# A graph layer's last stage: a place of its own for every chunk of x

## The chip, the core and the metric

The kernel runs on one core of a Trainium2 chip. A core has five engines with queues of their own: TensorE (PE, matrix products and transposes), VectorE (DVE), ScalarE (ACT), GpSimd (POOL, here the issuer of gathers) and SyncE (SP, here the issuer of plain loads and stores). 16 DMA engines move data between the device memory and the on-chip memory SBUF, which has 128 partitions. An issuing engine works through its queue in order: a load that has to wait for its place holds back all that stands behind it.

The metric is the time of one execution on the device, in microseconds (us).

## The reference

`x` is a table of 12,500 nodes with 256 float32 features; `src` and `dst` list 200,000 edges, sorted by `dst`.

```python
h = maximum(layernorm(x), 0)                      # per row, no scale or shift
agg = segment_sum(h[src], dst, num_segments=N)    # sum over incoming edges
z = (1 + eps_gin) * h + agg
t = relu(batchnorm(z @ W1 + b1, g1, bt1))         # 256 -> 512, statistics over all nodes
y = t @ W2 + b2                                   # 512 -> 256
out = x + relu(batchnorm(y + h, g2, bt2))         # statistics over all nodes
```

Each batch norm needs the whole table's mean and variance before one row of its result can be made. So the work falls into three stages: gather and first layer, second layer, and output.

## The kernel before, in words

The 12,500 rows are cut into 25 chunks of 512 rows (`chunks`; the last has 212). The transposed form of a chunk puts features on the partitions.

**First stage** (lines 341 to 600, an order written out by hand under `manual_schedule`). It normalizes rows of x, gathers rows by edge with indirect DMAs from GpSimd (line 435, 12 tiles of 128 edges to a group, 131 groups), sums them by destination with products against a 0/1 matrix (L464, L478), and forms the first product in slices (L514). The product goes untransformed to a device table `t_tab` (1 MB a chunk), its statistics into `st1`; the transposed h lies in a device table `h_cols`. Five landing places for gathered groups rotate. Two of them are permanent pairs `lands[k] = (gta, gtb)`, of 8 KB and 4 KB on each partition; the others, `gt`, come from a pool. `dstT` and `srcT` (6,656 bytes on each partition) hold the edges' target and source indices, `w1s` and `w2s` (4 KB each) the two weights. All of these are permanent.

**Second stage** (L623 to L642). For each chunk SP loads the stored product into `ti` (one of three buffers of 8 KB) and the transposed h into `yT[g]`, of which every chunk has its own. ScalarE applies batch norm and relu into `tT`, which lies in the two `gta` in turn; TensorE multiplies by `w2s` (L637, 16 matmuls a chunk), VectorE adds h (L641) and takes statistics (L642). The last chunk is worked ahead of the one before it.

**Last stage** (L654 to L672). For each chunk ScalarE applies the second batch norm (L657), TensorE transposes back (L663), VectorE adds the result onto the rows of x in place (L668), and SP stores them to `out` (`carry`, L328). The rows of x, 4 KB on each partition for a chunk, have been loaded before by SP (`x_rows`, L330).

Where the 25 chunks of x lie: chunks 0 to 7 in the pool `xin` (8 places), 8 and 9 in the two `gtb`, 10 to 15 in the pool `xmore` (6 places, in the space of the `ti` buffers). Chunks 16 to 23 reuse the places of 0 to 7, and chunk 24 that of chunk 16. Such a load waits until the store of the place's former chunk has landed; it is traced three chunks behind that store.

Outside the first stage the order on each queue is made by a planner at build time: it places what its model of time holds ready, the earlier line of the program first. A load whose place is free early can thus come ahead of loads that stand before it in the program. The two `gtb` loads did: their place was free when the gathers had ended.

The functions that the diff touches:

Of the kernel before, what the change touches and what calls it, by code (L numbers as in the profile page):

```python
# [7 lines left out]
F32 = mybir.dt.float32  # L8
# [6 lines left out]
P = 128  # L15
R = 4
# [4 lines left out]
LEAD = 30  # L21
EARLY = 2
LOW = 8
XAHEAD = 10
XMORE = 6


# [6 lines left out]
def kernel(  # L34
# [16 lines left out]
    nc = tc.nc  # L51
    N, D = x.shape
# [5 lines left out]
    NCH = -(-N // CH)  # L58
# [24 lines left out]
    def move(eng, sb, table, g, store):  # L83
# [23 lines left out]
    srcT = consts.tile([P, NBLK * P], I32, name="srcT")  # L107
    dstT = consts.tile([P, NBLK * P], F32, name="dstT")
# [6 lines left out]
    lands = [  # L115
        (consts.tile([P, LOW, D], F32, name=f"gta{k}"), consts.tile([P, GT - LOW, D], F32, name=f"gtb{k}"))
        for k in range(EARLY)
    ]
# [18 lines left out]
    w1s = consts.tile([P, DC, H], F32, name="w1s")  # L137
    w2s = consts.tile([P, HC, D], F32, name="w2s")
# [5 lines left out]
    at = 0  # L144
# [6 lines left out]
    with ExitStack() as es:  # L151
# [54 lines left out]
        place = raw.tile([P, NG], I32, name="place")  # L206
# [47 lines left out]
        at = 0  # L254
# [52 lines left out]
    def fast():  # L307

        parts = []
        for n0, w in chunks:  # L310
            n = w * R
            parts.append([(c, min(P, n - c * P)) for c in range(-(-n // P))])

        def pieces(g):

            whole = sum(rows == P for _, rows in parts[g])
            yield 0, whole, P
            for c, rows in parts[g][whole:]:
                yield c, c + 1, rows

        def carry(eng, sb, table, g, store):
            n0 = chunks[g][0]
            for c0, c1, rows in pieces(g):
                if c0 == c1:
                    continue
                side = table[n0 + c0 * P : n0 + (c1 - 1) * P + rows, :].rearrange("(c p) d -> p c d", p=rows)
                if store:
                    eng.dma_start(side, sb[:rows, c0:c1, :])  # L328
                else:
                    eng.dma_start(sb[:rows, c0:c1, :], side)  # L330

        with ExitStack() as fs:
            keep = fs.enter_context(tc.tile_pool(name="keep", bufs=1))

            h_cols = dram.tile([NCH, P, DC, CH], F32, name="h_cols")
# [5 lines left out]
            with ExitStack() as es:  # L341
# [188 lines left out]
                def first(c):  # L530

                    return min(i for i in range(NG) if c in reach(i))
# [11 lines left out]
                for c in range(NCH):  # L544
                    k = max(first(c) + 1, c + 2)
# [59 lines left out]
            late = fs.enter_context(tc.tile_pool(name="late", bufs=1, reuse_waits="tile"))  # L605
            yT = [late.tile([P, DC, w * R], F32, name=f"yT{g}") for g, (_, w) in enumerate(chunks)]

            xin = fs.enter_context(tc.tile_pool(name="xin", bufs=XAHEAD - EARLY, reuse_waits="tile"))
            xrs = []

            def x_rows(g):
                if g < NCH:
                    if XAHEAD - EARLY <= g < XAHEAD:
                        xrs.append(lands[g - XAHEAD + EARLY][1])
                    else:
                        pool = xmore if XAHEAD <= g < XAHEAD + XMORE else xin
                        xrs.append(pool.tile([P, R, D], F32, name="xr"))
                    carry(nc.sync, xrs[g], x, g, store=False)


            with tc.tile_pool(name="tin", bufs=3, side="right", reuse_waits="tile") as tin, tc.tile_pool(name="ps_y", bufs=4, space=PSUM) as ps_y:

                for k, g in enumerate([*range(NCH - 2), NCH - 1, NCH - 2]):  # L623
                    n = chunks[g][1] * R
                    ti = tin.tile([P, HC, CH], F32, name="ti")
                    nc.sync.dma_start(ti[:, :, :n], t_tab[g, :, :, :n])
                    nc.sync.dma_start(yT[g], h_cols[g, :, :, :n])
                    tT = lands[k % EARLY][0].rearrange("p a d -> p (a d)").rearrange("p (f n) -> p f n", n=CH)
                    for f in range(HC):
                        nc.scalar.activation(  # L630
                            tT[:, f, :n], ti[:, f, :n], AF.Relu, bias=of1[:, f : f + 1],
                            scale=sc1[:, f : f + 1],
                        )
                    for d in range(DC):
                        py = ps_y.tile([P, CH], F32, name="py")
                        for f in range(HC):
                            nc.tensor.matmul(  # L637
                                py[:, :n], lhsT=w2s[:, f, d * P : (d + 1) * P], rhs=tT[:, f, :n],
                                start=(f == 0), stop=(f == HC - 1),
                            )  # L640
                        nc.vector.tensor_add(yT[g][:, d, :], py[:, :n], yT[g][:, d, :])  # L641
                        nc.vector.bn_stats(st2[:, d, g, :], yT[g][:, d, :])  # L642
                for g in range(XAHEAD):
                    x_rows(g)

            sc2, of2 = norm(late, st2, mv2, DC, g2c, bt2c, b2c, "2")

# [1 line left out]
            with tc.tile_pool(name="xmore", bufs=XMORE, side="right", reuse_waits="tile") as xmore, tc.tile_pool(  # L649
                name="ps_o", bufs=3, space=PSUM  # L650
            ) as ps_o:
                for g in range(XAHEAD, XAHEAD + XMORE):
                    x_rows(g)
                for g in range(NCH):  # L654
                    xt = xrs[g]
                    for d in range(DC):
                        nc.scalar.activation(  # L657
                            yT[g][:, d, :], yT[g][:, d, :], AF.Relu, bias=of2[:, d : d + 1], scale=sc2[:, d : d + 1]
                        )
                    po = ps_o.tile([P, R, D], F32, name="po")  # L660
                    for c, rows in parts[g]:
                        for d in range(DC):
                            nc.tensor.transpose(  # L663
                                po[:rows, c, d * P : (d + 1) * P], yT[g][:, d, c * P : c * P + rows], ident
                            )
                    for c0, c1, rows in pieces(g):
                        if c0 < c1:
                            nc.vector.tensor_add(xt[:rows, c0:c1, :], po[:rows, c0:c1, :], xt[:rows, c0:c1, :])  # L668
                    carry(nc.sync, xt, out, g, store=True)

                    if g >= 3:
                        x_rows(g - 3 + XAHEAD + XMORE)  # L672

    def general():

# [214 lines left out]
    with tc.If(off == 0):  # L890
        fast()
# [32 lines left out]
```

## Time and profile before

| | |
|---|---|
| median of 3 runs | 2235.57 us (2233.42 to 2241.05) |
| the profiled execution | 2235.88 us |
| its span, first to last instruction | 2233.7 us |
| mean granted TensorE clock | 0.834 |

| stretch, us | what | TensorE busy | ScalarE busy | share of the DMA engines | GB/s |
|---|---|---|---|---|---|
| 0 to 1960 | first stage: gathers | 1249.45 us | 387.88 us | | |
| 1960 to 2000.5 | first stage's end | 31.23 us | 8.25 us | 0.29 | 98 |
| 2000.5 to 2170.2 | second stage | 169.63 us | 78.76 us | 0.67 | 239 |
| 2170.2 to 2178.2 | second batch norm, first output chunk | 3.49 us | 4.88 us | 0.22 | 71 |
| 2178.2 to 2233.7 | last stage from its first store on | 24.85 us | 30.29 us | 0.92 | 312 |

A line of the profile names an engine, a line of the kernel (L657 is line 657), the tile written and, behind an arrow, what is read. "x6" is a count. PE is TensorE's matmuls; SPq is the SP queue, where the time of a DMA line is that of its issue, not of its transfer. "Idle" stands with what ended it: `[0.82 <-DMA ...]` says that the engine waited 0.82 us and a DMA released it. The chain that ended last is followed back from the last instruction, at each step to what released it. The share of the DMA engines is a mean over 16; values over 1 come from transfers that overlap on one engine.

### The profile page before, as it was taken

Reading aid. Unit: us, or ns where it says so; the run is one execution under the profiler, and the core shown is the slowest. Engines: PE = TensorE matmul, PEld = TensorE weight load, DVE = VectorE, ACT = ScalarE, POOL = GpSimd, SP = SyncE. Lnnn points to the kernel's source line nnn. Section 1 sums busy time; section 2 is a strip of 40 time slices with the busy share of each in tenths; the row PEclk is TensorE's granted clock in tenths of the full one; section 3 lists DMA queues with packets and bytes.
Section 4 is the critical chain, followed back from the end, with each engine's and each line's share of the span. In section 5 each row is a group of like instructions: output and inputs, shape, how many; then the busy total and the mean of one; then the engine's idle time right before and its main releaser. Section 6 shows DMA issues by size and latency. Waiting matters only on the chain.

```text
span 2233.7 us, 15142 instructions
## 1 busy us (share of the span) xinstructions
PE 1478.6 (66%) x4874; PEld 1066.5 (48%) x4874; DVE 716.5 (32%) x1092; ACT 510.1 (23%) x963; POOL 1480.4 (66%) x1575
## 2 busy tenths in 40 slices
PE   3567677667666666656666666666666666679994
PEld 2455545545444544544454444444444544444443
DVE  5566656531222122122212221211221121124345
ACT  4666666520000000000000000000000000034445
POOL 7777777777777777777777777777777777700000
PEclk9888888888888788878877887888887788789998
DMA  6677767644444444444444444444443444438739
GB/s 196 208 228 232 246 218 237 183 128 120 129 128 129 116 128 129 120 123 129 131 116 125 132 120 125 129 117 126 129 133 113 126 128 118 130 131 320 252 118 311
DMA packets 157615, 349.47 MB, mean 156 GB/s; under 512 B 30104, under 2 KB 82452, under 8 KB 154454
## 3 DMA queue, kind: packets, MB, share of 16 engines
q0 software_dynamic: 75008, 204.90, 32.8%
q1 hardware_dynamic: 54224, 104.03, 13.9%
q10 hardware_dynamic: 28294, 39.47, 4.9%
q8 instruction: 41, 0.67, 0.1%
q14 instruction: 48, 0.39, 0.1%
HBM read 284.28 MB, written 64.00 MB: 156 GB/s over the span
## 4 chain that ended last, share of the span: by engine, by line
POOL 52%; issue 22%; PE 11%; ACT 6%; DVE 4%; DMA 4%; ACTq 0%; SPq 0%; DVEq 0%; POOLq 0%
POOL gt L435 32%; POOL gta L435 12%; PE py L637 8%; POOL gtb L435 6%; DMA gt<-in_x_dram,srcT 3%; ACT gt L381 2%; DVE stg L370 2%; PE ps L478 2%; PE ph L514 1%; ACT yT L657 1%; ACT gta L381 1%; DMA out_dram<-xr 1%; DVE oh L464 1%; POOL gta L212 1%; ACT gtb L381 0%
## 5 line engine op out<-in xcount | busy, mean ns | idle before, releaser
L478 PE MATMUL ps<-gt,oh 128*128 128x256 f32 x1872 | 577.0, 481 | 402.5 <-DMA gt<-h_tab,srcT 321.5
L435 POOL DMA_INDIRECT gt<-h_tab,srcT x720 | 680.7, 945 | 219.3 <-issue 219.3
L478 PEld LDWEIGHTS ps<-gt,oh 128*128 128x128 f32 x1872 | 459.1, 250 | 546.0 <-issue 315.7
L478 PE MATMUL ps<-gta,oh 128*128 128x256 f32 x838 | 291.9, 524 | 270.5 <-DMA gta<-h_tab,srcT 212.1
L478 PEld LDWEIGHTS ps<-gta,oh 128*128 128x128 f32 x838 | 224.8, 275 | 352.4 <-issue 198.3
L525 DVE BATCH_NORM_STATS2 st<-ph 128x6 f32<-128x512 f32 (+1 forms) x100 | 68.4, 684 | 971.2 <-PE ph L514 971.2
L435 POOL DMA_INDIRECT gta<-h_tab,srcT x323 | 305.2, 945 | 98.4 <-issue 95.9
L527 ACT COPY ts<-ph 128x512 f32<-128x512 f32 (+1 forms) x100 | 57.4, 574 | 1326.5 <-DVE st L525 1326.5
L435 POOL DMA_INDIRECT gt<-in_x_dram,srcT x216 | 204.2, 945 | 65.8 <-issue 60.9
L464 DVE TENSOR_TENSOR oh<-col,dstT 128x1536 f32<-128x1536 f32 x131 | 227.7, 1738 | 0.0
L514 PE MATMUL ph<-zc,w1s 128*128 128x512 f32 (+1 forms) x400 | 193.1, 610 | 20.6 <-DVE hc L423 20.1
L507 DVE TENSOR_TENSOR zc<-pz,zc 128x512 f32<-128x512 f32 (+8 forms) x187 | 93.9, 520 | 282.5 <-PE pz L496 244.2
L435 POOL DMA_INDIRECT gtb<-h_tab,srcT x160 | 151.2, 945 | 48.7 <-issue 47.5
L637 PE MATMUL py<-gta,w2s 128*128 128x512 f32 (+1 forms) x400 | 169.6, 587 | 3.7 <-ACT gta L630 3.7
L496 PE MATMUL pz<-at,zs 128*128 128x256 f32 x524 | 134.9, 380 | 5.0 <-ACT zs L485 5.0
L637 PEld LDWEIGHTS py<-gta,w2s 128*128 128x128 f32 x400 | 76.4, 192 | 96.4 <-issue 75.7
L514 PEld LDWEIGHTS ph<-zc,w1s 128*128 128x128 f32 x400 | 78.3, 199 | 79.8 <-issue 49.1
L381 ACT ACTIVATE gt<-gt,nbg,rsg 128x256 f32<-128x256 f32 x216 | 108.1, 586 | 9.1 <-DVE nbg L379 8.1
L496 PEld LDWEIGHTS pz<-at,zs 128*128 128x128 f32 x524 | 97.6, 190 | 19.1 <-ACT zs L485 7.1
L630 ACT ACTIVATE gta<-ti,of,sc 128x512 f32<-128x512 f32 (+1 forms) x100 | 79.6, 803 | 82.9 <-PE py L637 78.8
L478 PE MATMUL ps<-gtb,oh 128*128 128x256 f32 x416 | 98.3, 379 | 0.0
L435 POOL DMA_INDIRECT gta<-in_x_dram,srcT x80 | 75.6, 946 | 24.4 <-issue 8.5
(97 smaller groups left out, 897.3 us busy)
## 6 DMA issues: line engine op xcount, KB each, us to landing
t_tab<-ts ACTq DMA_DIRECT2D x96, 256.0 KB
ti<-t_tab SPq DMA_DIRECT2D x24, 1024.0 KB
xt<-in_x_dram SPq DMA_DIRECT2D x24, 512.0 KB
h_tab<-ht ACTq DMA_DIRECT2D x24, 512.0 KB
h_cols<-hc SPq DMA_DIRECT2D x24, 512.0 KB
zc<-h_cols SPq DMA_DIRECT2D x24, 512.0 KB
yT<-h_cols SPq DMA_DIRECT2D x24, 512.0 KB
gt<-h_tab,srcT POOLq DMA_INDIRECT x720, 2.8
```

Of the source, the lines that this page charges most:

```text
L370: nc.vector.bn_stats(st[:, c : c + 2, :].rearrange("p c s -> p (c s)"), two.rearrange("p c d -> p d c"),)
L381: nc.scalar.activation(slot(to, c), slot(v, c), AF.Relu, bias=nb[:, c : c + 1], scale=rs[:, c : c + 1])
L435: nc.gpsimd.indirect_dma_start(out=slot(ga, t - t0)[:rows], out_offset=None, in_=x if i < LEAD else h_tab, in_offset=bass.IndirectOffsetOn ...
L464: nc.vector.tensor_tensor(ohs[i][:, :n, :], col[:, :P].unsqueeze(1).to_broadcast([P, n, P]), dstT[:, t0 : t0 + n].unsqueeze(2).to_broadcas ...
L478: nc.tensor.matmul(ps, lhsT=oh[:rows, j, :], rhs=slot(ga, j)[:rows], start=(j == 0), stop=(j == n - 1))
L496: nc.tensor.matmul(pz[:, d, :], lhsT=zs[:, d * P : (d + 1) * P], rhs=at, start=True, stop=True)
L507: nc.vector.tensor_add(side, pz[:, :, a - lo : b - lo], side)
L514: nc.tensor.matmul(ph[:, :n], lhsT=w1s[:, d, f * P : (f + 1) * P], rhs=zc[c][:, d, :n], start=(d == 0), stop=(d == DC - 1),)
L525: nc.vector.bn_stats(st1[:, f, c, :], ph[:, :n])
L527: nc.scalar.copy(ts[:, :n], ph[:, :n])
L630: nc.scalar.activation(tT[:, f, :n], ti[:, f, :n], AF.Relu, bias=of1[:, f : f + 1], scale=sc1[:, f : f + 1],)
L637: nc.tensor.matmul(py[:, :n], lhsT=w2s[:, f, d * P : (d + 1) * P], rhs=tT[:, f, :n], start=(f == 0), stop=(f == HC - 1),)
```

## The change

All 25 chunks of x now have a place of their own, and no load of x waits for a store.

- Chunks 0 to 7 stay in `xin`, 8 and 9 in the two `gtb`.
- Chunks 10, 11 and 12 lie in `dstT`, `srcT` (taken as float32) and `w1s`; the last chunk, 24, in the rest of `dstT`.
- All of these loads are traced after the second stage's loop, as the ten of before were, but within `issue_after(begun)`: on SP they stand behind the load of `yT` for the third chunk. This is an order of issue, no wait for a landing.
- Chunks 13 to 18 lie in `xmore`.
- Chunks 19 to 22 lie in the halves of the two `gta`, that of the second-to-last worked chunk first; chunk 23 in `w2s`. Their loads are traced right behind those of `xmore`, ahead of the output loop.
- The refill at the end of each turn of the output loop is gone.

```diff
-XAHEAD = 10
+XIN = 8
 XMORE = 6
...
-            xin = fs.enter_context(tc.tile_pool(name="xin", bufs=XAHEAD - EARLY, reuse_waits="tile"))
-            xrs = []
-
-            def x_rows(g):
-                if g < NCH:
-                    if XAHEAD - EARLY <= g < XAHEAD:
-                        xrs.append(lands[g - XAHEAD + EARLY][1])
-                    else:
-                        pool = xmore if XAHEAD <= g < XAHEAD + XMORE else xin
-                        xrs.append(pool.tile([P, R, D], F32, name="xr"))
-                    carry(nc.sync, xrs[g], x, g, store=False)
+            xin = fs.enter_context(tc.tile_pool(name="xin", bufs=XIN, reuse_waits="tile"))
+            xrs = {}
+
+            def rows_in(flat, at=0, c=R):
+                return flat[:, at : at + c * D].rearrange("p (c d) -> p c d", d=D)
+
+            def x_rows(places):
+                for g, place in places:
+                    xrs[g] = place
+                    carry(nc.sync, place, x, g, store=False)
...
-                    nc.sync.dma_start(yT[g], h_cols[g, :, :, :n])
+                    landing = nc.sync.dma_start(yT[g], h_cols[g, :, :, :n])
+                    if k == 2:
+                        begun = landing.ins
...
-                for g in range(XAHEAD):
-                    x_rows(g)
+                behind = [lands[k][1] for k in range(EARLY)]
+                behind += [rows_in(dstT), rows_in(srcT.bitcast(F32)), rows_in(w1s.rearrange("p a b -> p (a b)"))]
+                with tc.issue_after(begun):
+                    x_rows([(g, xin.tile([P, R, D], F32, name="xr")) for g in range(XIN)])
+                    x_rows(enumerate(behind, XIN))
+                    x_rows([(NCH - 1, rows_in(dstT, R * D, len(parts[NCH - 1])))])
...
-                for g in range(XAHEAD, XAHEAD + XMORE):
-                    x_rows(g)
+                got = len(xrs) - 1
+                x_rows([(g, xmore.tile([P, R, D], F32, name="xr")) for g in range(got, got + XMORE)])
+                last = [lands[k][0][:, c : c + R, :] for k in reversed(range(EARLY)) for c in range(0, LOW, R)]
+                last += [rows_in(w2s.rearrange("p a b -> p (a b)"))]
+                assert got + XMORE + len(last) == NCH - 1
+                x_rows(enumerate(last, got + XMORE))
...
                     carry(nc.sync, xt, out, g, store=True)
-
-                    if g >= 3:
-                        x_rows(g - 3 + XAHEAD + XMORE)
```

## The prediction

> **What bounds the kernel now.** I read the chain that ended last in order of time, then the SyncE (SP) queue's own timeline, then the load of the DMA engines in chosen windows. The chain past 2000 us (start us, us, what):
>
> ```profile
> 2000.51 169.65 PE py L637 x400
> ...
> 2201.49 15.93 DMA out_dram<-xr x2
> 2217.43 2.96 DMA xr<-in_x_dram
> ```
>
> TensorE alone sets the second layer: 169.65 us without a gap, up to 2170.2. After it the chain is DMA: a 15.93 us wait for a store to land, then the load that takes its place. The queue that issues both (start us, us taken by the issues):
>
> ```profile
> 1902.93 17.32 SPq L330 DMA_DIRECT2D gtb<-in_x_dram  x2
> 1984.64 5.99 SPq L627 DMA_DIRECT2D yT<-h_cols  x3
> 2002.60 0.32 SPq L626 DMA_DIRECT2D ti<-t_tab  x1
> ...
> 2161.34 3.98 SPq L330 DMA_DIRECT2D xr<-in_x_dram  x6
> 2178.23 5.50 SPq L328 DMA_DIRECT2D out_dram<-xr  x4
> ...
> 2200.22 1.22 SPq L330 DMA_DIRECT2D xr<-in_x_dram  x1
> 2201.49 12.22 SPq L328 DMA_DIRECT2D out_dram<-xr  x8
> ...
> 2218.35 8.31 SPq L328 DMA_DIRECT2D out_dram<-xr  x7
> ```
>
> Loads and stores alternate from 2183 to 2201. Seven stores stand behind the load of 2217.43, the last chunk's, which waits for the store of the chunk that held its place. The windows (stretch, busy time by engine, granted clock, share of the 16 DMA engines, GB/s):
>
> ```profile
> core 0 of [0], span 2233.7 us
> 2017.00:2100.00 83.00, 83.00 (x195) 36.84 (x194) 33.86 (x49) 39.19 (x49) 0.00 (x0) 1.00 0.88 319
> 2100.00:2161.00 61.00, 61.00 (x146) 27.41 (x145) 24.18 (x36) 27.98 (x36) 0.00 (x0) 1.00 0.33 111
> 2164.00:2170.00 6.00, 6.00 (x15) 2.45 (x13) 2.32 (x4) 0.00 (x0) 0.00 (x0) 1.00 1.07 351
> 2172.00:2178.00 6.00, 3.29 (x14) 3.00 (x15) 2.43 (x8) 4.68 (x8) 0.00 (x0) 0.53 0.01 2
> 2178.00:2229.50 51.50, 25.05 (x184) 20.02 (x182) 28.83 (x26) 30.49 (x44) 0.00 (x0) 0.83 0.99 337
> 2180.00:2184.00 4.00, 3.36 (x27) 2.66 (x26) 4.00 (x4) 4.00 (x7) 0.00 (x0) 1.00 0.94 314
> 2184.00:2188.00 4.00, 3.05 (x24) 2.34 (x23) 3.46 (x4) 4.00 (x7) 0.00 (x0) 1.00 0.91 248
> 2188.00:2200.00 12.00, 9.46 (x72) 7.57 (x72) 10.52 (x9) 12.00 (x18) 0.00 (x0) 1.00 1.09 385
> 2210.00:2218.00 8.00, 0.00 (x0) 0.00 (x0) 0.51 (x1) 0.00 (x0) 0.00 (x0) 0.71 1.09 383
> 2218.00:2220.00 2.00, 0.00 (x0) 0.00 (x0) 0.00 (x0) 0.00 (x0) 0.00 (x0) 0.50 0.67 205
> 2220.00:2228.00 8.00, 0.00 (x0) 0.00 (x0) 0.75 (x2) 0.00 (x0) 0.00 (x0) 0.50 1.02 342
> ```
>
> From 2178 on the DMA engines are full (0.99), while no compute engine is. Before that they have room: 0.33 in 2100 to 2161, and nothing moves in 2172 to 2178. So the tail is bound by bytes, and some of them could have moved earlier.
>
> **The change part by part.** Sizes and compute pace:
>
> ```profile
> ti<-t_tab SPq DMA_DIRECT2D x24, 1024.0 KB
> xr<-in_x_dram SPq DMA_DIRECT2D x22, 512.0 KB
> yT<-h_cols SPq DMA_DIRECT2D x1, 212.0 KB
> ```
>
> ```profile
> 2173.61 34.87 ACT L657 ACTIVATE yT<-yT,of,sc 128x512 f32<-128x512 f32 x50 [0.82 <-DVE of L284]
> 2176.98 1.23 DVE L668 TENSOR_TENSOR xr<-po,xr 128x1024 f32<-128x1024 f32 x1 [3.40 <-PE po L663]
> 2209.29 1.23 DVE L668 TENSOR_TENSOR xr<-po,xr 128x1024 f32<-128x1024 f32 x1 [0.82 <-DMA out_dram<-xr]
> 2220.51 0.75 DVE L668 TENSOR_TENSOR xr<-po,xr 128x256 f32<-128x256 f32 x2 [10.00 <-DMA xr<-in_x_dram]
> ```
>
> *Refills removed.* Nine loads leave the tail: eight of 512 KB and the last chunk's 212 KB (as large as its yT), 4.41 MB. Check: stores of 12.80 MB (12,500 rows of 1 KB) and these make 17.21 MB; the tail's 51.5 us at 337 GB/s are 17.4 MB. At 337 they are worth 13.1 us.
>
> *Two gtb loads moved, three and the last added.* Chunks 8 and 9 went out at 1902.93 to 1920; now they stand behind the third yT load, issued near 1990. Chunks 10, 11, 12 and 24 join them. That is 2.84 MB into a stage that reads at 319 GB/s with TensorE busy 83 of 83 us, and has a third of its DMA in use from 2100 on. Cost taken: 0; without that cover, 2.84 MB at 351 GB/s is 8.1 us. Below nothing it cannot go, since TensorE has no idle time there to win. Their issues (26 x-load DMAs before and after) are short beside a chunk's period.
>
> *Five late loads.* Six xmore loads go out at 2161.34, as before. The halves of gta1, those of gta0, and w2s follow. Their readers end with the second-to-last chunk, and with TensorE's last matmul at 2170.2. These 2.62 MB need 7.5 us at 351 GB/s. The first six fill the engines till about 2171.8 (nothing moves past 2172), so the five are in by 2179.3, mostly in the dead stretch 2172 to 2178. Cost: stores, first issued at 2178.23, move from 2179.3, some 1 us.
>
> *Wait removed.* The load of 2217.43 no longer blocks SP. The DMA gap that it leaves is 2 us at 205 GB/s where 383 stood, 0.9 us; it goes with the refills, and the last add (2220.51) can follow the one of 2209.29 directly.
>
> *Wait added.* `issue_after` is an order on SP alone; behind it stand only x loads. The late loads wait for TensorE's end with the stores queued behind them, but the first store is ready 8 us later. The places in dstT, srcT and w1s have readers that all end with the first layer, before 2000. No instruction of TensorE, VectorE, ScalarE or GpSimd is added or taken away; the same 26 adds run with the same shapes, so these edits cost 0.
>
> *The tail rebuilt.* The open price is the rate of stores with no loads among them. The rows give 314 at first (2180 to 2184), 383 with a deep queue (2210 to 2218) and 342 at the end. ScalarE hands over rows in 34.87 us, 367 GB/s, so a queue builds only if stores run slower than that. I take 314 from 2179.3 to 2188 (2.73 MB) and 383 for the other 10.07 MB (26.3 us): the last bytes at 2214.3. In the trace they stop at about 2229.5 and the span ends at 2233.7, 4.2 later: 2218.5. Bounds: all at 383 (33.4 us) gives 2216.9. By SP: adds end at 2209.29 + 1.23 + 0.75 = 2211.3 at the latest, and the last two stores' issue took up to 2.76 us, 7.05 us before the end:
>
> ```profile
> 2223.89 2.76 SPq L328 DMA_DIRECT2D out_dram<-xr  x2
> ```
>
> That gives 2221.1. Between the two I take 2219.5, nearest the rebuilt 2218.5 and leaning to SP's path because short final stores can queue. Against the span of 2233.7 that is 14.2 us less. The profiled execution took 2235.88 (2.2 beside its span), 0.3 above the median of 2235.57: so 2221.7 for it, and 2221.4 for the median.
>
> Rows of 383 and 385 GB/s bear on a rule: the Trainium skill, "SBUF — State Buffer", section "Summary: rules for kernel authors", would estimate HBM to SBUF transfers at about 358 GB/s. With it the stores would take 35.8 us instead of 33.4, and the lower bound of the span would be 2219.3, not 2216.9. The trace does not agree with it as a cap: 385 stood for 12 us.
>
> **The rivals.**
> *A: stores alone do not fill the engines.* For: 314 and 248 GB/s in the first 8 us of storing, at shares of 0.94 and 0.91. Against: 383 for 8 us at 2210 to 2218, when by the order of the queue all but the last load had been served. At their mean, 281, for all 12.80 MB: 45.6 us, span 2229.1, time 2231.0, 0.2% faster. It takes the gain only if 281 lasts for the whole stage. In this direction points the Trainium skill, "DMA: Bandwidth & Descriptors", section "Anatomy of one DMA", with a fixed 2.0 us for each DMA beside bytes at 436 GB/s: paid in turn that estimate is 3.2 us for 512 KB and some 80 us for 26 stores, but the row of 383 GB/s (1.37 us for 512 KB) shows queued stores not paying it in turn.
>
> *B: the early x loads go ahead of t and yT loads and TensorE starves.* The order behind the third yT load is a planner's; from 1990 to 2002.60 SP was idle, so it may fill that hole. Fourteen places hold 7.03 MB, 20.0 us at 351; from about 1995 they run to 2015, then the load of 2002.60 and its yT (1.57 MB, 4.5 us) and 2.96 us to land make 2022.5.
>
> ```profile
> 2020.59 1.68 ACT L630 ACTIVATE gta<-ti,of,sc 128x512 f32<-128x512 f32 x2 [3.46 <-PE py L637]
> ```
>
> The fourth chunk's activation began at 2020.59, so the stall is about 2 us, to 10 if the loads start late; it decides from a bulk ending after 2013. Taken at 6: 2227.4. Against: program order has t and yT ahead, and before all yT loads went out first.
>
> *C (slower): two chunks in one tile are tracked as one.* Then the second half of each gta tile loads only after the first half's chunk is stored. A chunk takes ScalarE 1.43 us (34.87 by 24.4 chunks), and the first add ends 3.2 us behind its activations (2178.21 against 2175.04), so chunk 19's ends near 2173.61 + 20 x 1.43 + 3.2 = 2205.4; its store lands 15.93 later, load 2.96, add 1.23: 2225.5. Store 21 then lands and chunk 22 loads (2.96 each, 1.3 for two issues at 3.98 by 6), add 1.23: 2234.0; an issue, 1.25 MB at 342 (3.7 us) and 4.2 to the end: 2242.6, time 2244.5. It decides once the two waits exceed the 14 us won. Against: gathers write eight slots of one gta tile, and do not wait for each other:
>
> ```profile
> L435 POOL DMA_INDIRECT gta<-h_tab,srcT x323 | 305.2, 945 | 98.4 <-issue 95.9
> ```
>
> **How the numbers follow.** Forecast 0.73; A 0.08; B 0.09; C 0.06; 0.04 for what I cannot name, half of it slower. Over 0.3% (6.7 us, about what a measurement tells from no change): the forecast, 0.06 of B and 0.01 make faster 0.80; A, the rest of B and 0.01 make 0.12; C and 0.02 make slower 0.08. The likeliest case's own range is 2217.5 (all at 383, less the runs' spread of 2 us) to 2225. The range reaches up through B to 2230, short of A.
>
> **What would show it.** Right: no x load on SP after 2178; 13 places and the last chunk loaded in some 14 issues between 1990 and 2115; five more behind the six of 2161; TensorE's 169.65 us unchanged; 26 stores in a row, some 1.4 us apart; DMA idle gone from 2172 to 2178, and full until 2214. Wrong: stores under 300 GB/s throughout (A), TensorE waiting at 2005 to 2025 (B), an x load on SP that waits for a store (C), or the first store issued clearly after 2180.

## The result and the profile after

The changed kernel takes 2224.39 us (median of 6 runs, 2221.64 to 2226.28), the kernel before 2235.31 us (6 runs). The ratio is 0.9948 with a 95% interval of 0.9935 to 0.9962: 0.52% faster, some 11 us. On a second chip, where both kernels' first stage takes some 300 us longer, the ratio was 0.9951 (0.9935 to 0.9967).

The profiled execution is the fastest of the six, 2221.64 us. Its chain in order of time (start us, us, what):

```profile
core 0 of [0], span 2219.7 us
...
1998.22 169.65 PE py L638 x400
...
2180.51 17.80 ACT yT L666 x26
...
2207.51 0.74 DVE dstT L677 x2
```

The second layer has its 169.65 us again. It ends at 2167.87, 2.3 us earlier than before, because of a shorter first stage, in which nothing was changed. What the change is worth is read from that point on: 63.5 us to the end of the span before (2170.16 to 2233.7), 51.8 us now. That is 11.7 of the 14.0 us between the two spans. The waits on landed stores are gone from the chain, which now runs through ScalarE and VectorE to the last add, at 2208.25. The chain is followed back from the last instruction of an engine, so it doesn't show what sets the end: the stores behind that add, which keep the DMA engines full until 2214.

The SP queue after the change (start us, us taken by the issues):

```profile
2063.35 1.80 SPq L626 DMA_DIRECT2D yT<-h_cols  x3
2070.16 0.98 SPq L330 DMA_DIRECT2D xr<-in_x_dram  x2
...
2104.98 1.23 SPq L330 DMA_DIRECT2D dstT<-in_x_dram  x2
...
2159.05 3.81 SPq L330 DMA_DIRECT2D xr<-in_x_dram  x6
2162.90 6.57 SPq L330 DMA_DIRECT2D gta<-in_x_dram  x4
2169.52 1.31 SPq L330 DMA_DIRECT2D w2s<-in_x_dram  x1
2175.72 9.69 SPq L328 DMA_DIRECT2D out_dram<-xr  x8
...
2209.24 2.85 SPq L328 DMA_DIRECT2D out_dram<-dstT  x2
```

All yT loads go out first, then the early x loads, from 2070 to 2106. The late ones stand in 2159 to 2171, and from 2175.72 on SP issues stores alone. The windows (busy time by engine, granted clock, share of the DMA engines, GB/s):

```profile
2100.00:2161.00 61.00, 61.00 (x153) 28.70 (x152) 25.49 (x38) 28.30 (x36) 0.00 (x0) 1.00 0.40 136
2168.00:2176.00 8.00, 3.44 (x17) 3.19 (x18) 4.27 (x10) 4.97 (x8) 0.00 (x0) 0.82 1.10 349
2172.00:2178.00 6.00, 5.44 (x33) 5.19 (x33) 3.05 (x3) 6.00 (x10) 0.00 (x0) 0.72 1.10 353
2180.00:2184.00 4.00, 3.23 (x24) 2.51 (x24) 3.47 (x4) 4.00 (x6) 0.00 (x0) 1.00 1.02 346
2188.00:2200.00 12.00, 9.13 (x68) 7.15 (x68) 10.48 (x9) 12.00 (x18) 0.00 (x0) 1.00 1.04 341
2200.00:2214.00 14.00, 5.53 (x43) 4.27 (x41) 7.31 (x8) 6.20 (x10) 0.00 (x0) 0.88 1.04 340
2214.00:2215.50 1.50, 0.00 (x0) 0.00 (x0) 0.00 (x0) 0.00 (x0) 0.00 (x0) 0.50 0.65 191
```

The stretch in which nothing moved, 2172 to 2178, now carries 353 GB/s; the first stores stand in its last 2.3 us, and the late loads alone make 349 from 2168 to 2176. The stores start at 346 instead of 314, but they never reach the 383 to 385 GB/s of before: they run at 340 to the end. The engines are full (1.02 to 1.04) at a lower rate.

### The profile page after: what moved, and what is told of

Read it like the earlier page. It is cut to its first block, busy times and chain, and to the rows that moved or that the text cites. A ratio compares the mean times of both kernels' runs of the same rounds, so it can differ in the third digit from the quotient of the medians.

```text
span 2219.7 us, 15131 instructions
## 1 busy us (share of the span) xinstructions
PE 1479.0 (67%) x4874; PEld 1065.5 (48%) x4874; DVE 715.7 (32%) x1092; ACT 509.9 (23%) x963; POOL 1481.3 (67%) x1575
## 4 chain that ended last, share of the span: by engine, by line
POOL 51%; issue 22%; PE 12%; ACT 6%; DMA 4%; DVE 3%; ACTq 0%; DVEq 0%; POOLq 0%
POOL gt L435 32%; POOL gta L435 12%; PE py L638 8%; POOL gtb L435 6%; DMA gt<-in_x_dram,srcT 3%; PE ps L478 3%; ACT gt L381 2%; ACT yT L666 1%; PE ph L514 1%; DVE stg L370 1%; ACT gta L381 1%; DMA gta<-in_x_dram,srcT 1%; POOL gta L212 1%; ACT gtb L381 0%; DVE oh L464 0%
```

## The experiments

The measure is the time from the second layer's last matmul (start and length of its row in the chain) to the end of the span, called the tail here. The first stage differs between chips and runs; this stretch hardly does. The experiments ran on three chips whose first stage is the longer one: the two parts, the deep queue and the 4 KB runs on one, the two kernels again, the paired activations and the kernel without the order on a second, the rest on a third. Tails are compared across them. That of the changed kernel was 51.8 and 52.1 us in two traces, that of the kernel before 63.5 and 61.6, so a difference of 2 us or less between single traces is weak evidence by itself; the rates in the windows are the firmer one.

**The two kernels again.** No edit; the kernel before and the changed one on the same chip.

> The changed kernel itself, beside the others of this call. From the end of the second layer to the end of its span 51.8 us is expected, as in its first trace; against the kernel before 0.9935 to 0.9962 where the first stage takes as long as in the first traces, and the same 11 to 12 us in any case, since both kernels share that stage.

> The kernel before itself, for its trace: from the end of the second layer to the end of the span 63.5 us as in its first trace. If that were nearer to 60 here, the separate gains of the early and the late places would have been read too high.

The chain and two windows of the kernel before on that chip:

```profile
core 0 of [0], span 2544.5 us
...
2313.30 169.64 PE py L637 x400
```

```profile
2503.00:2526.00 23.00, 14.75 (x109) 11.42 (x107) 17.15 (x14) 18.29 (x27) 0.00 (x0) 0.98 1.09 383
2530.00:2538.00 8.00, 0.00 (x0) 0.00 (x0) 0.75 (x2) 0.00 (x0) 0.00 (x0) 0.50 1.00 340
```

And of the changed one:

```profile
core 0 of [0], span 2534.3 us
...
2311.90 170.35 PE py L638 x400
```

```profile
2494.00:2526.00 32.00, 21.15 (x156) 16.55 (x155) 25.23 (x23) 26.60 (x39) 0.00 (x0) 0.98 1.04 344
```

The tail of the kernel before is 61.6 us here (63.5 in its first trace), that of the changed one 52.1 (51.8). So the change is worth 9.5 to 11.7 us in the tail. The two rates repeat: 383 GB/s while loads and stores alternate and some time behind, 344 with stores alone.

**One part alone.** First the early places only:

```diff
-                last = [lands[k][0][:, c : c + R, :] for k in reversed(range(EARLY)) for c in range(0, LOW, R)]
-                last += [rows_in(w2s.rearrange("p a b -> p (a b)"))]
-                assert got + XMORE + len(last) == NCH - 1
-                x_rows(enumerate(last, got + XMORE))
+                more = got + XMORE
...
                     carry(nc.sync, xt, out, g, store=True)
+                    if g >= 3 and more + g - 3 < NCH - 1:
+                        x_rows([(more + g - 3, xin.tile([P, R, D], F32, name="xr"))])
```

> Only the early places are kept: chunks 10 to 12 and 24 lie in dstT, srcT and w1s; the five late places are undone, and chunks 19 to 23 refill the places of chunks 0 to 4 after their stores. 2.62 MB of loads stand among the stores. Measured from the end of the second layer to the end of the span (63.5 us before, 51.8 after). Theory 'bytes' (each MB taken out of the tail is worth the same, 11.7 us by 4.41 MB = 2.65 us): 58.8 us. Theory 'mixed traffic is faster' (loads and stores together move at 385 GB/s, stores alone at 343, so a refill costs less than its bytes): about 55.8. Theory 'only the blocked last load mattered' (its wait on SP is gone here as well): 52 to 53.

The chain's row of the second layer, and two windows:

```profile
core 0 of [0], span 2523.9 us
...
2297.32 169.64 PE py L638 x400
```

```profile
2487.00:2507.00 20.00, 14.77 (x109) 11.42 (x107) 17.46 (x16) 18.30 (x27) 0.00 (x0) 1.00 1.09 383
2511.00:2519.00 8.00, 0.00 (x0) 0.00 (x0) 0.00 (x0) 0.00 (x0) 0.00 (x0) 0.50 1.03 336
```

Then the late places only:

```diff
-                behind = [lands[k][1] for k in range(EARLY)]
-                behind += [rows_in(dstT), rows_in(srcT.bitcast(F32)), rows_in(w1s.rearrange("p a b -> p (a b)"))]
-                with tc.issue_after(begun):
-                    x_rows([(g, xin.tile([P, R, D], F32, name="xr")) for g in range(XIN)])
-                    x_rows(enumerate(behind, XIN))
-                    x_rows([(NCH - 1, rows_in(dstT, R * D, len(parts[NCH - 1])))])
+                x_rows([(g, xin.tile([P, R, D], F32, name="xr")) for g in range(XIN)])
+                x_rows(enumerate([lands[k][1] for k in range(EARLY)], XIN))
...
                     carry(nc.sync, xt, out, g, store=True)
+                    if g >= 3 and more + g - 3 < NCH:
+                        x_rows([(more + g - 3, xin.tile([P, R, D], F32, name="xr"))])
```

> Only the late places are kept: ten chunks early and six in xmore as before the change, chunks 16 to 20 in the two gta and in w2s, and chunks 21 to 24 refill the places of 0 to 3. 1.79 MB of loads stand among the stores. From the end of the second layer to the end of the span: 'bytes' 56.5 us; 'mixed traffic is faster' about 54; 'only the blocked last load mattered' 52 to 53.

The same rows:

```profile
core 0 of [0], span 2506.4 us
...
2282.37 169.53 PE py L638 x400
```

```profile
2472.00:2488.00 16.00, 12.18 (x91) 9.45 (x89) 13.89 (x12) 16.00 (x24) 0.00 (x0) 1.00 1.09 386
2492.00:2500.00 8.00, 0.00 (x0) 0.00 (x0) 0.28 (x1) 0.00 (x0) 0.00 (x0) 0.61 1.04 346
```

Tails: 56.9 us with the early places, 54.5 with the late ones. Against the changed kernel's 52, refills of 2.62 MB cost 4.9 us and refills of 1.79 MB cost 2.5; all 4.41 MB of before cost 9.5 on the second chip. Each of the two is 1.9 to 2.0 us below what "bytes" had forecast, and nearest to "mixed traffic is faster" (55.8 and 54). That forecast had taken 63.5 us as the tail of before. With the 61.6 and 52.1 of the repeated traces "bytes" comes to 57.7 and 56.0 and "mixed" to about 56 and 54.3: the late places still speak for "mixed", the early ones (56.9) stand halfway between. "Only the blocked last load mattered" (52 to 53) falls in both. So no part alone holds the gain, and the parts seem to add up to more than the whole: 4.7 and 7.1 us against the 61.6 of before, where both together give 9.5 (the tail of before is from another chip, and it was 63.5 once; the comparison with the changed kernel is the firmer one). The rows offer a reason: among loads, and for some time behind them, the stores move at 383 to 386 GB/s, without them at 336 to 346. As ratios to the kernel before the parts are 0.9965 (0.9947 to 0.9983) and 0.9968 (0.9951 to 0.9986), which do not tell the one from the other.

**What makes the stores faster beside loads.** A deep queue was the first suspect:

```diff
...
-                    carry(nc.sync, xt, out, g, store=True)
+                gone = carry(nc.sync, xrs[NCH - 1], out, NCH - 1, store=True)
+                with tc.issue_after(gone.ins):
+                    for g in range(NCH - 1):
+                        carry(nc.sync, xrs[g], out, g, store=True)
```

> The changed kernel, but all stores stand on SP behind the store of the last chunk, so 12.58 MB are queued at once with no load near them. It tells what let the stores of before move at 383 GB/s at 2210 to 2218, while those of the changed kernel move at 343. Theory 'deep queue': the stores alone run at 380 or more, 33 us from the first to the last byte. Theory 'loads mixed in': 343 GB/s, 37 us. The first store goes out some 40 us after the second layer's end, so the span is some 30 us longer; that is no verdict on the change.

A window with stores alone:

```profile
2511.00:2543.00 32.00, 0.00 (x0) 0.00 (x0) 0.00 (x0) 0.00 (x0) 0.00 (x0) 0.50 1.04 340
```

340 GB/s for 32 us with stores waiting in the queue all the time: depth is not it. Next, loads moved among the stores, without any wait on a landed store:

```diff
...
-                x_rows(enumerate(last, got + XMORE))
+                held = list(enumerate(last, got + XMORE))
+                x_rows(held[:2])
+                xrs.update(dict(held[2:]))
...
-                    carry(nc.sync, xt, out, g, store=True)
+                    gone = carry(nc.sync, xt, out, g, store=True)
+                    if 3 <= g < 6:
+                        with tc.issue_after(gone.ins):
+                            x_rows([held[g - 1]])
```

> The changed kernel, but the loads of chunks 21, 22 and 23 stand on SP behind the stores of chunks 3, 4 and 5; no load waits for a store to land. The same bytes move, in another order. Theory 'mixed traffic is faster, and stores behind it stay fast': 385 GB/s from about 16 us after the second layer's end for at least 15 us, where the changed kernel has 340; the dead stretch before the first store costs 1.57 MB (4.5 us) and the faster stores win 2.4 to 4 us back, so the end stands 51 to 54 us behind the second layer. Theory 'what made the stores fast was the wait on a landed store': 340 GB/s throughout, 56 us.

The last load on SP, the chain's row of the second layer, and two windows:

```profile
core 0 of [0], span 2535.6 us
...
2498.06 0.67 SPq L330 DMA_DIRECT2D w2s<-in_x_dram  x1
```

```profile
2311.01 169.65 PE py L639 x400
```

```profile
2501.00:2512.00 11.00, 8.56 (x64) 6.85 (x64) 9.62 (x8) 11.00 (x17) 0.00 (x0) 1.00 1.09 384
2517.00:2529.00 12.00, 2.28 (x19) 1.73 (x17) 3.67 (x5) 2.00 (x4) 0.00 (x0) 0.75 1.04 343
```

Three loads among the stores, the last issued at 2498.06, and 384 GB/s stand until 2512; then the stores fall back to 343, over some 5 us. So no wait is needed for the fast stretch. The tail is 54.9 us, 1 us past the range that I had given for "mixed" and 1 short of the other theory's 56, so the rate decides here and not the tail. The bytes left for later cost more than the fast stretch gives back. Last, whether any load does it:

```diff
...
-                    carry(nc.sync, xt, out, g, store=True)
+                    gone = carry(nc.sync, xt, out, g, store=True)
+                    if 3 <= g < 11:
+                        at = (R + 2) * D + (g - 3) * 16
+                        with tc.issue_after(gone.ins):
+                            nc.sync.dma_start(dstT[:, at : at + 16], x[g * P : (g + 1) * P, :16])
```

> The changed kernel with eight small loads added (64 bytes to a partition, 8 KB each, into dead columns of dstT), one behind each of the stores of chunks 3 to 10. They add next to no bytes. Theory 'any load among the stores brings the engines into the fast state': 385 GB/s after them, end 48 to 49 us behind the second layer's end. Theory 'only real load traffic does': 340 GB/s, 52 us.

The chain's row of the second layer, and a window of the stores:

```profile
core 0 of [0], span 2523.8 us
...
2301.50 170.75 PE py L639 x400
```

```profile
2492.00:2516.00 24.00, 15.04 (x112) 11.65 (x110) 18.02 (x17) 18.58 (x28) 0.00 (x0) 0.99 1.04 339
```

339 GB/s and a tail of 51.6 us: eight small loads do nothing. Three loads of 512 KB do bring the faster rate; whether their bytes, their runs (1 KB against 64 bytes) or something else about them counts was not separated. In the run before this one the rate stood for 14 us behind the issue of the last load (2498.06 to 2512). Part of that is the queue: a store issued at 2209.12 in the first trace of the kernel before landed 8.3 us later. Why the effect goes on behind that stays open.

**The order behind the third yT load.**

```diff
-                with tc.issue_after(begun):
+                if begun:
```

> The changed kernel without the order behind the third yT load. The planner then puts the loads into srcT and dstT among the loads of zc in the first stage, and those into gtb ahead of the first yT. Theory 'the order is only a safeguard': the second layer has its 169.6 us and the end stands 51.8 us behind it. Theory 'rival B of the prediction' (early x loads get in the way): TensorE waits in the first stage for zc or in the second for t, 2 us or more.

Two early x loads on SP, and the chain's row of the second layer:

```profile
core 0 of [0], span 2523.8 us
...
1522.52 0.38 SPq L330 DMA_DIRECT2D dstT<-in_x_dram  x1
...
2247.15 0.35 SPq L330 DMA_DIRECT2D dstT<-in_x_dram  x1
```

```profile
2302.90 169.65 PE py L638 x400
```

Loads into dstT go out from 1522 on, in the middle of the first stage, ahead of all yT loads. The second layer keeps its 169.65 us (from 2302.90) and the tail is 51.3 us. In this one run the order is a safeguard only: none of TensorE's waits was ended by a load of zc, and the whole span is shorter than that of the changed kernel on the same chip (2534.3).

**Longer runs, and the better kernel.** In the store-bound tail the next lever is the rate. Four neighbouring rows to a partition make runs of 4 KB:

```diff
...
+            def carry4(sb, table, g, store):
+                if chunks[g][1] < P:
+                    return carry(nc.sync, sb, table, g, store=store)
+                n0 = chunks[g][0]
+                side = table[n0 : n0 + CH, :].rearrange("(p c) d -> p c d", c=R)
...
-                            nc.tensor.transpose(
-                                po[:rows, c, d * P : (d + 1) * P], yT[g][:, d, c * P : c * P + rows], ident
-                            )
+                            cols = yT[g][:, d, c * P : c * P + rows]
+                            if chunks[g][1] == P:
+                                cols = yT[g][:, d, :].rearrange("f (p c) -> f c p", c=R)[:, c, :]
+                            nc.tensor.transpose(po[:rows, c, d * P : (d + 1) * P], cols, ident)
...
```

> The changed kernel, but in the last stage a partition holds four neighbouring rows of x and out, so that a chunk moves in runs of 4 KB and not of 1 KB (the transposes read every fourth column; the last chunk stays as it was). In the second layer's loads, with runs of 4 and 8 KB, 426 GB/s stood at 2005 to 2010 before. Theory 'length of the runs sets the rate': loads and stores at 400 GB/s or more, the tail follows ScalarE's 34.9 us, span 3 to 4 us shorter than the changed kernel's. Theory 'stores alone are capped at 343 whatever the runs': no change. If the transposes with a stride are slower than ScalarE's 1.41 us a chunk, TensorE takes over and the stage gets longer.

The chain's row of the second layer, a window, and ScalarE's group of instructions (busy us, mean ns, idle before and what ended it):

```profile
core 0 of [0], span 2512.9 us
...
2295.59 169.64 PE py L648 x400
```

```profile
2480.00:2505.00 25.00, 21.28 (x139) 17.98 (x139) 21.81 (x18) 23.61 (x35) 0.00 (x0) 1.00 0.96 382
```

```profile
L676 ACT ACTIVATE yT<-yT,of,sc 128x512 f32<-128x512 f32 (+1 forms) x50 | 34.9, 798 | 0.8 <-DVE of L284 0.8
```

The tail is 47.7 us, 4 less than the changed kernel's, and the ratio to the kernel before 0.9941 (0.9918 to 0.9964). The DMA engines are no longer full (0.96 where the changed kernel has 1.04), while ScalarE works as long as in the kernel before (34.9 us) and is busy for 23.6 us of the window's 25: that points to ScalarE as the bound. So its activations were made on two chunks at once (here against the 4 KB kernel's lines):

```diff
-            yT = [late.tile([P, DC, w * R], F32, name=f"yT{g}") for g, (_, w) in enumerate(chunks)]
+            pairs = [late.tile([P, DC, 2 * CH], F32, name=f"yT{j}") for j in range(NCH // 2)]
+            yT = [pairs[g // 2][:, :, g % 2 * CH : g % 2 * CH + CH] for g in range(NCH - 1)]
...
-                    for d in range(DC):
+                    wide = yT[g] if g < 2 or g == NCH - 1 else pairs[g // 2]
+                    for d in range(DC if g < 2 or g % 2 == 0 else 0):
...
```

> The kernel with 4 KB runs, and ScalarE's last activations made on two chunks at once (1,024 columns; the first two chunks and the last stay single). In the 4 KB trace ScalarE's 1.41 us a chunk sets the pace of the last stage, with TensorE at 1.23 and VectorE at 1.23 us a chunk and the DMA engines at 0.95. Theory 'ScalarE is the bound': a pair takes 1.15 us for each half of the features in place of 1.40 in two, the stage runs at 1.25 to 1.30 us a chunk, and the end of the span comes 2.5 to 3 us earlier: 45 us from the end of the second layer, where the 4 KB kernel has 47.7. Theory 'the stores are the bound again': at 407 GB/s 1.29 us a chunk, so at least 46.

> The kernel with 4 KB runs and paired activations once more, against the kernel before: its last stage has 46.3 us from the second layer's end where the changed kernel has 52 and the kernel before 61.6 to 63.5, so a ratio of 0.993 to 0.994 is expected, whatever the first stage takes.

ScalarE's group, the chain's row and a window of the first of the two runs:

```profile
L679 ACT ACTIVATE yT<-yT,of,sc 128x1024 f32<-128x1024 f32 (+1 forms) x26 | 27.8, 1161 | 0.8 <-DVE of L284 0.8
```

```profile
2305.19 169.64 PE py L650 x400
```

```profile
core 0 of [0], span 2521.1 us
...
2488.00:2514.00 26.00, 20.20 (x149) 18.39 (x148) 22.66 (x22) 19.05 (x19) 0.00 (x0) 0.94 1.02 402
```

ScalarE needs 27.8 us (without the last chunk's two), the stores run at 402 GB/s, and the tails of the two runs are 46.3 us (2474.83 to 2521.1) and 46.1: the DMA engines are full again (1.02), at the faster rate. The 2.5 to 3 us of the first theory did not come; the second, with at least 46 us, fits. The 1.4 to 1.6 us gained on the 4 KB kernel lie between single traces on different chips, so what the pairing itself is worth is not shown. The ratios to the kernel before are 0.9938 (0.9916 to 0.9959) and 0.9943 (0.992 to 0.9965). On the same chip the changed kernel's median is 2531.89 us, this version's 2525.49. Against the kernel before it is clearly faster; against the changed kernel the intervals of the two ratios overlap, and the evidence is the tail, 46 us against 52.

## Why the prediction was right, and what was off

**Direction and mechanism: right.** The tail was bound by its transfers, and the refills could move into stretches where the DMA engines had room. Each marker came as forecast: no x load on SP once the stores begin, 14 chunks early, the late five behind those of xmore, the dead stretch filled, TensorE's 169.65 us untouched, 26 stores in a row.

**The size: 11 us instead of 14.** The profiled execution's 2221.64 us lies next to the 2221.4 forecast, but by luck: 2.3 us of it come from the first stage. The median is 3 us above. The tail, forecast at 49.3 us (2170.2 to 2219.5), took 51.8. The term that was mis-sized is the rate of the stores in "the tail rebuilt": 314 GB/s for 8.7 us, then 383 for the remaining 10.07 MB, 26.3 us. It measured 346 at first and 340 to 341 from 2188 on, 29.6 us for the same bytes, 3.3 us more, of which the better start gives about 0.8 back. The row behind the 383 (2210 to 2218) did show stores alone; what I had not seen is that it needs loads shortly before. The 342 GB/s at 2220 to 2228, which I put down to a shallow queue, was the rate of stores by themselves, as the experiment with all stores queued at once showed (340).

As a rate, the estimate that I had set aside was nearer than my 383: the Trainium skill, "SBUF — State Buffer", section "Summary: rules for kernel authors", has about 358 GB/s for transfers between HBM and SBUF. Stores of 1 KB runs alone made 340. Its span of 2219.3 means a tail of 49.1 us, though, also short of the 51.8 measured. As a cap the figure does not hold in these runs: 383 to 386 stood with loads among the stores, 402 with runs of 4 KB.

**A row misread: the 15.93 us.** The prediction calls the chain's "15.93 DMA out_dram<-xr x2" a wait for a store to land. "x2" says that it is two stores in turn, of 7.63 and 8.30 us. The second, and SP's own wait for it (us in total, times, longest):

```profile
2209.12 8.30 DMA out_dram<-xr
```

```profile
SPq L330 <- DMA out_dram<-xr: 3.6, 1, 3.6
```

A store lands 8.3 us after its issue here, and SP stood still for 3.6 us. The forecast doesn't use the 15.93, but rival C does: with 8.30 its span is 2235.0 and not 2242.6, so it would have been about no change and not slower.

**Early loads at no cost: right.** They stand from 2070 to 2106, behind all yT loads, under a TensorE that is busy throughout. Rival B did not come about, and not without the order either.

**Late loads: right.** They fill the stretch ahead of the first store (349 GB/s from 2168 to 2176), and that store goes out 7.9 us behind the second layer (8.1 before).

**The price of the refills: too high.** 13.1 us was their bytes at 337 GB/s; taking them away brought 9.5 to 11.7. With them went the fast stretch that comes with loads among the stores.

**Rival A** had the direction and not the mechanism: stores alone do fill the engines (a share of 1.04), but at 340 GB/s, between its 281 and my 383. The fixed 2.0 us for each DMA that stands beside it comes from a section of the Trainium skill ("DMA: Bandwidth & Descriptors", "Anatomy of one DMA") that fits it to DMAs issued from GpSimd. These stores go out from SP, and at 340 GB/s a queued one took 1.54 us, not the estimate's 3.2. **Rival C** fell: the four loads into the halves of gta follow one another from 2162.90, and none waits for a store.

## What to carry to other kernels

Price a transfer stage by a row that has the same traffic in it: a rate measured while loads and stores alternate says nothing certain of the stores once the loads are moved away. When transfers are the bound, look at the length of the contiguous runs as well as at their place in the order: going from 1 KB to 4 KB took 4 us from this stage, after the moved loads had taken 9.5 to 11.7. Before you price a wait by a row of the chain, see whether the row is several pieces in one. And read a small gain from the stretch that was changed, since the first stage alone varied by some 2 us between two profiled executions.

## What the hardware showed that was not expected

- Stores in runs of 1 KB moved at 336 to 346 GB/s by themselves, also with a queue that never ran dry (340), and at 383 to 386 with loads of 512 KB among them. The faster rate went on for 10 us and more behind the last such load's issue (e.g. to 2512 with the last issued at 2498.06; some 8 us of that may be the load's own time in the queue), then fell back with no visible event. Eight loads of 8 KB did not bring it about (339). The cause is open.
- With runs of 4 KB the stores alone made 402 GB/s. The Trainium skill, "DMA: Bandwidth & Descriptors", section "Specifications", gives 512 B as the smallest transfer for line rate. The runs here differ: four times the length of 1 KB still gained 18%.
